# Layer 3's dense part: a chunk's attention values read from PSUM behind the last elementwise sum of the chunk ahead of it

## The chip, the cores and the metric

The kernel runs on one core of a Trainium2 chip. A core has engines that work side by side, each through its own queue of instructions: TensorE (PE in the profile; its weight loads are shown as PEld), VectorE (DVE), ScalarE (ACT), GpSimd (POOL), and SyncE (SP), which here only issues transfers. An engine starts its instructions in the order of its queue; one that waits for another engine holds back everything behind it. The metric is the device time of one execution in microseconds (us), lower is better. The number before is a median of 3 runs.

## The reference, cut to what matters

A graph of 2708 nodes with 512 features goes through four layers; each normalises the rows, clips them at zero, computes something over the graph and adds it to the rows. The change lies where layer 2 ends and layer 3 begins:

```python
    # --- layer 2 (adj_preln) ---
    h = jnp.maximum(_layernorm(x, axis=-1), 0.0)
    x = x + _L2_gnn_ref(h, adj, ...)       # attention with 8 heads of 64, softmax, then elu
    # --- layer 3 (adj_preln) ---
    h = jnp.maximum(_layernorm(x, axis=-1), 0.0)
    x = x + _L3_gnn_ref(h, adj, ...)
    # _L3: agg = mask @ x / max(deg, 1);  self_f = x @ W_self + b_self;  nb_f = agg @ W_nb + b_nb
    #      relu(concat([self_f, nb_f]) @ W_comb + b_comb)
```

The attention's weighted sums and the softmax's denominators are there at this point, transposed, in DRAM. What is left of layer 2 per node is the division, `elu`, and the addition to `x`; what begins of layer 3 is the normalisation and two products with 512x512 matrices (W_self and W_nb, each already multiplied by its half of W_comb).

## The kernel before, in words

The 2708 rows are cut into 22 chunks of 128 rows (the last has 20). The last part of layer 2 and the dense part of layer 3 are one software pipeline over these chunks, here called the dense loop. For a chunk c its steps are:

- `load3`: SyncE's queue loads the chunk's attention sums (aT), denominators (sT) and rows (x).
- `turn3`: TensorE multiplies sT into `sums_ps` (L1249) and transposes aT in four pieces into `av_ps` (L1253), both in PSUM. VectorE then makes the reciprocal denominators in four small instructions (`rs`, L1255 to L1258) and takes the attention values out of PSUM, multiplied by them, into `y` (L1260). These five are the instructions that the change touches.
- `elu3`: GpSimd makes z = min(y, 0) (L1267). VectorE adds max(y, 0) to the rows (L1268). ScalarE makes tanh(z/2) over y (L1270) and exp(z) over z (L1271); since exp(z) - 1 = (exp(z) + 1) tanh(z/2), VectorE multiplies these (L1272) and adds the product to the rows (L1273). L1273 is the last elementwise sum of a chunk: it completes layer 2.
- `save3`: ScalarE's queue stores the finished rows (L101).
- `normalize3`: VectorE takes mean and variance (L219, L221), ScalarE the square root (L223), VectorE its reciprocal (L225) and the normalised rows `hn` (L235).
- `transpose3`: TensorE transposes hn into PSUM (`hT_ps`, L246), ScalarE clips it at zero on the way out (L248).
- `nb3` and `self3`: TensorE multiplies hT with the two matrices (L187, eight matmuls of 512 columns each). Of nb3's result ScalarE takes the upper half of the bits (`halves`, L299), VectorE the rest (L300). To self3's result VectorE adds the bias (L1291), and ScalarE's queue stores it.

The first chunks run through these steps already between the last steps of the attention, by a plan that is written out by hand. The rest runs in this loop:

```python
        for c in range(1, NC):
            nb3(c)
            do(transpose3, c + 1)
            do(turn3, c + 3)
            do(normalize3, c + 2)
            do(save3, c + 2)
            do(elu3, c + 3)
            do(load3, c + 5)
            final = self3(c)
```

So at one time three chunks are in work on VectorE: c+3 comes out of the attention, c+2 gets its elu and its normalisation, c its product's halves. Square root on one side and tanh and exponential on the other need different tables on ScalarE, so each chunk has two loads of a table (shown as ACT_TABLE_LOAD); tanh is tied behind the newest square root by `issue_after(roots[-1])`.

The order in which one engine's instructions stand in its queue is not that of the source. The framework plays the program through before it runs, and gives an engine that becomes free the earliest traced instruction whose inputs are there by its own estimate of times. `tc.issue_after(ins)` is the means to correct this: what is traced within the block stands behind `ins` in the queue of `ins`'s engine. It adds an order, not a signal between engines. In the dense loop SBUF tiles of the pool `e3` (aT, sT, rs, y3, z3) have two buffers each, and PSUM eight banks.

Behind the dense loop comes the sum over the graph (`aggregate`, matmuls of L425), which runs to the end.

Of the kernel before, what the change touches and what calls it, by code (L numbers as in the profile page):

```python
# [15 lines left out]
ALU = mybir.AluOpType  # L16
# [6 lines left out]
R = 128  # L23
# [17 lines left out]
TINY = 1.0e-30  # L41
# [3 lines left out]
def fast_layers(  # L45
# [36 lines left out]
    nc = tc.nc  # L82
    N, D = x_in.shape
    H, _, O = w2.shape
# [876 lines left out]
    er = late.tile([R, NC, H], F32, name="er")  # L961
# [262 lines left out]
    tails_w = tails.tile([P, len(middle), O + S], F32, name="tails_w")  # L1224
    nc.gpsimd.memset(tails_w, 0.0)
    tails_f = tails.tile([P, 3], F32, name="tails_f")
    kept3, h3, l3_weights = {}, {}, []


    def load3(c):  # L1230
# [15 lines left out]
    def turn3(c):  # L1246
        xc, aT, sT = kept3[c]
        pr = ps.tile([P, 2, H], F32, name="sums_ps", tag="ps")
        nc.tensor.matmul(pr[:R], sT, mix[:NS], start=True, stop=True)  # L1249
        pt = ps.tile([P, H, O], F32, name="av_ps", tag="ps")  # L1250
        flat = pt.rearrange("p h o -> p (h o)")
        for k in range(NF):
            nc.tensor.transpose(flat[:R, k * P : (k + 1) * P], aT[:, k, :], ident)  # L1253
        rs = e3.tile([R, H, 1], F32, name="rs")
        nc.vector.tensor_tensor(rs[:, :, 0], er[:, c], pr[:R, 0], ALU.mult)  # L1255
        nc.vector.tensor_tensor(rs[:, :, 0], rs[:, :, 0], pr[:R, 1], ALU.add)
        nc.vector.tensor_scalar(rs[:, :, 0], rs[:, :, 0], TINY, None, op0=ALU.max)
        nc.vector.reciprocal(rs[:, :, 0], rs[:, :, 0])  # L1258
        y = e3.tile([R, H, O], F32, name="y3")
        nc.vector.tensor_tensor(y, pt[:R], rs.to_broadcast([R, H, O]), ALU.mult)  # L1260
        kept3[c] = xc, y.rearrange("p h o -> p (h o)")

    def elu3(c):

        xc, y = kept3[c]
        z = e3.tile([R, D], F32, name="z3")
        nc.gpsimd.tensor_scalar(z, y, 0.0, None, op0=ALU.min)  # L1267
        nc.vector.scalar_tensor_tensor(xc[:R], y, 0.0, xc[:R], op0=ALU.max, op1=ALU.add)  # L1268
        with tc.issue_after(roots[-1]):
            nc.scalar.activation(y, z, AF.Tanh, scale=0.5)  # L1270
            nc.scalar.activation(z, z, AF.Exp)  # L1271
        nc.vector.scalar_tensor_tensor(z, z, 1.0, y, op0=ALU.add, op1=ALU.mult)  # L1272
        nc.vector.tensor_tensor(xc[:R], xc[:R], z, ALU.add)  # L1273
        kept3[c] = xc

    def save3(c):
# [169 lines left out]
    for at_step, fn, c in (  # L1446
        (20, load3, 0),
        (19, load3, 1),
        (16, turn3, 0),
        (16, elu3, 0),  # L1450
        (15, load3, 2),
        (12, normalize3, 0),
        (12, save3, 0),
        (11, turn3, 1),
        (10, load3, 3),
        (10, elu3, 1),
        (7, normalize3, 1),
        (7, save3, 1),
        (6, transpose3, 0),
        (4, nb3, 0),  # L1460
        (4, turn3, 2),
        (3, self3, 0),
        (3, load3, 4),
        (3, elu3, 2),
        (2, transpose3, 1),
        (1, turn3, 3),
        (1, normalize3, 2),
        (1, save3, 2),
        (1, elu3, 3),
        (1, load3, 5),  # L1470
    ):
        behind(len(steps) - at_step, fn, c)
# [708 lines left out]
def kernel(tc: tile.TileContext, *args: bass.AP):  # L2181

    nc = tc.nc
    with tc.tile_pool(name="verdict", bufs=1) as pool:
        verdict = pool.tile([1, 1], I32, name="verdict")
        fast_layers(tc, *args, verdict)
        odd = nc.values_load(verdict[0:1, 0:1], min_val=0, max_val=P + 1)
        with tc.If(odd > 0):
            general_layers(tc, *args)
# [32 lines left out]
```

## Time and profile before

| | us |
|---|---|
| median of 3 runs | 1746.12 (1745.71 to 1747.05) |
| the profiled execution's own time | 1746.28 |
| its span, from the first to the last instruction | 1744.5 |
| TensorE busy in the span | 1721.5 |
| VectorE busy | 1317.9 |
| ScalarE busy | 845.4 |
| GpSimd busy | 248.3 |
| the dense loop, from its first product (nb3 of chunk 1) to the first matmul of the sum behind it | 1357.20 to 1522.14 |
| mean granted TensorE clock | 0.998 |

The busy shares are means over the whole kernel. The timeline gives an instruction's start, its duration, engine, line and names; in brackets the time that its engine stood idle before it, and what ended this. The chain of waits goes back from the last instruction through what released each step; it shows which engine's work followed on which, and where two engines take turns.

### The profile page before, as it was taken

The page shows a single profiled execution, that of the slowest core. Times are in us where ns is not written, and L with a number is a line of the kernel's source. Part 1 is how long each engine was busy: PE and PEld are TensorE (multiplying, and loading weights), DVE is VectorE, ACT ScalarE, POOL GpSimd, SP SyncE. Part 2 cuts the span into 40 slices and gives each one's busy share as a digit, 9 for nine tenths or more (in the row PEclk, how much of TensorE's full clock was granted, in tenths as well). Part 3 has the DMA queues.
Part 4 walks back from the last instruction along what each step waited for, and adds up shares of the span by engine and source line. Part 5 has one row for each costly group of instructions (what it writes and reads, how often), then busy time and mean ns, then how long its engine had stood idle before and what let it go on. Part 6 is the DMA issues. An engine that isn't in the chain of part 4 may idle for free.

```text
span 1744.5 us, 29430 instructions
## 1 busy us (share of the span) xinstructions
PE 1721.5 (99%) x11280; PEld 1074.9 (62%) x11280; DVE 1317.9 (76%) x1902; ACT 845.4 (48%) x1556; POOL 248.3 (14%) x252
## 2 busy tenths in 40 slices
PE   8999999999999999999999999999999999999998
PEld 5567777744458888644675665433434544588886
DVE  7759889865555556888899999999999787633334
ACT  5446767622210000266878888888794656400000
POOL 1003323311111111365000000000001222100000
PEclk9999999999999999999999999999999999999999
DMA  8446666444551111342420221022022444313221
GB/s 292 136 122 198 205 204 188 139 115 124 121 142 49 49 49 53 118 129 94 131 64 15 61 64 47 26 65 66 16 68 77 135 132 128 113 36 109 74 73 41
DMA packets 167227, 177.37 MB, mean 102 GB/s; under 512 B 84127, under 2 KB 106591, under 8 KB 166060
## 3 DMA queue, kind: packets, MB, share of 16 engines
q1 hardware_dynamic: 144428, 131.99, 27.4%
q10 hardware_dynamic: 18808, 33.37, 5.0%
q0 software_dynamic: 3840, 10.03, 1.5%
q8 instruction: 90, 1.47, 0.4%
q14 instruction: 61, 0.50, 0.1%
HBM read 111.64 MB, written 55.36 MB: 96 GB/s over the span
## 4 chain that ended last, share of the span: by engine, by line
PE 42%; DVE 9%; issue 3%; ACT 2%; DMA 2%; SPq 1%; POOL 0%; ACTq 0%; DVEq 0%; POOLq 0%
PE av L1315 15%; PE acc L425 12%; DVE t L1070 7%; PE self_ps L187 4%; PE nb_ps L187 4%; PE sums L1315 3%; DMA x<-x 1%; PE hT_ps L246 1%; PE wh_ps L187 1%; DVE wh_a L1117 1%; ACT b L1088 1%; PE av_ps L1253 1%; DVE f L1134 1%; DVE ln_st L219 0%; DMA rb<-rT 0%
## 5 line engine op out<-in xcount | busy, mean ns | idle before, releaser
L1070 DVE SCALAR_TENSOR_TENSOR t<-rb,ec,vT 128x2708 f32<-128x2708 f32 (+2 forms) x214 | 510.8, 2456 | 8.3 <-PE sums L1315 6.4
L1315 PE MATMUL av<-t,whs 128*32 128x451 f32 (+5 forms) x4432 | 444.6, 514 | 6.0 <-DVE t L1070 4.7
L425 PE MATMUL acc<-halves,kt 128*128 128x512 f32 x1848 | 423.6, 390 | 1.0 <-DVE kt L873 1.0
L425 PEld LDWEIGHTS acc<-halves,kt 128*128 128x128 f32 x1848 | 346.1, 188 | 75.3 <-DVE kt L873 2.6
L1088 ACT ACTIVATE b<-t,eb 128x2708 bf16<-128x2708 f32 (+1 forms) x119 | 285.1, 2396 | 33.2 <-DVE t L1070 33.1
L1315 PEld LDWEIGHTS av<-t,whs 128*32 128x32 f32 (+1 forms) x4432 | 192.4, 110 | 169.6 <-issue 119.4
L425 PE MATMUL acc<-halves,ar 128*128 128x512 f32 x924 | 243.8, 414 | 0.0
L425 PEld LDWEIGHTS acc<-halves,ar 128*128 128x128 f32 x924 | 172.5, 188 | 58.3 <-issue 20.8
L223 ACT ACTIVATE ln_rs<-ln_mv,eps 128x1 f32<-128x1 f32 x88 | 25.7, 295 | 305.9 <-DMA x<-x 199.0
L873 DVE SCALAR_TENSOR_TENSOR kt<-lastr,index,vT 128x512 fp32r<-128x512 int16 (+3 forms) x154 | 112.8, 747 | 72.4 <-PE acc L425 72.2
L1539 DVE CAST kt<-vT 128x512 fp32r<-128x512 uint8 (+3 forms) x154 | 56.4, 368 | 130.6 <-PE acc L425 130.6
L1267 POOL TENSOR_SCALAR z<-y 128x512 f32<-128x512 f32 x22 | 43.7, 1987 | 628.7 <-DVE y L1260 623.1
L558 DVE TENSOR_TENSOR_SCAN cum<-ai,deg 128x512 int16<-128x512 int32 (+2 forms) x110 | 128.3, 1170 | 0.0
L601 ACT ACTIVATE cum<-cum,limit 128x512 int16<-128x512 int16 (+3 forms) x132 | 88.0, 667 | 51.5 <-DVE deg L566 49.4
L1315 PE MATMUL sums<-t,whs 128*32 128x325 f32 (+4 forms) x952 | 103.9, 449 | 0.0
L1054 ACT ACTIVATE whs<-wh,ef 128x64 f32<-128x64 f32 x214 | 72.5, 341 | 53.0 <-PE sums L1315 18.9
L219 DVE BATCH_NORM_STATS2 ln_st<-x 128x6 f32<-128x512 f32 x88 | 60.5, 689 | 49.7 <-DMA x<-x 35.1
L187 PE MATMUL wh_ps<-w2s,hT 128*128 128x512 f32 x168 | 76.0, 595 | 0.9 <-ACT hT L248 0.9
L187 PE MATMUL h_ps<-w0s,hT 128*128 128x512 f32 x168 | 76.5, 598 | 0.0
L1315 PE MATMUL sums<-b,parts 128*32 128x338 bf16 (+2 forms) x884 | 76.2, 308 | 0.0
L552 ACT ACTIVATE ar<-ai 128x512 fp32r<-128x512 int32 (+2 forms) x132 | 75.0, 568 | 1.8 <-DMA ai<-in_adj 1.3
L187 PE MATMUL self_ps<-wfs,hT 128*128 128x512 f32 x168 | 75.7, 593 | 0.0
(211 smaller groups left out, 1956.2 us busy)
## 6 DMA issues: line engine op xcount, KB each, us to landing
x<-x SPq DMA_DIRECT2D x105, 256.0 KB
ai<-in_adj SPq DMA_DIRECT2D x84, 256.0 KB
x<-x ACTq DMA_DIRECT2D x84, 256.0 KB
x<-in_x SPq DMA_DIRECT2D x42, 256.0 KB
rb<-rT SPq DMA_DIRECT2D x7, 1354.0 KB
wh<-whd SPq DMA_DIRECT2D x63, 96.0 KB
packed<-two POOLq DMA_DIRECT2D x44, 128.0 KB, 3.0
whd<-wh SPq DMA_DIRECT2D x21, 256.0 KB
```

The costliest lines, as they stand in the source:

```text
L187: nc.tensor.matmul(po[:n], lhsT[:, f, :n], w[:, f, :], start=(f == 0), stop=(f == NF - 1))
L219: nc.vector.bn_stats(st[:n], xc[:n])
L425: nc.tensor.matmul(acc[:R], weight[:, k * R : (k + 1) * R], parts[:, i, :], start=(m == 0 and i == 0), stop=(m == NC - 1),)
L552: nc.scalar.activation(ar[:, :gw], ai[:, :gw], AF.Square, accum_out=squares[:R, m, g : g + 1])
L558: nc.vector.tensor_tensor_scan(cum[:n, :gw], ai[:n, :gw], ai[:n, :gw], 0.0 if g == 0 else deg[:n, m : m + 1], op0=ALU.add, op1=ALU.max,)
L601: nc.scalar.activation(cum[:n, :gw], cum[:n, :gw], AF.Sign, bias=limit[:n], scale=-1.0, accum_out=signs[:n, m, g : g + 1],)
L873: nc.vector.scalar_tensor_tensor(by_chunk(kt, cs), lastr[:, cs[0] * R : (cs[-1] + 1) * R].rearrange("p (c r) -> p c r", r=R), index[:R, m ...
L1054: ins = nc.scalar.activation(t[:q, :O], wh.pop((u, m))[:q], AF.Copy, scale=by)
L1070: ins = nc.vector.scalar_tensor_tensor(t[:q, : hi - lo], row[h][:q, lo:hi], ec[:q, m, h : h + 1], vT[g][:q, k, lo:hi], op0=ALU.max, op1=AL ...
L1088: nc.scalar.activation(b[:q, : hi - lo], weight[s][:, : hi - lo], AF.Sigmoid, bias=eb[:q, m, h : h + 1], scale=STEEP,)
L1315: nc.tensor.matmul(p[j * S : (j + 1) * S, : b - a], lhsT, rhs[:, part * size + a : part * size + b], start=(s % NC == 0), stop=(s % NC == ...
L1539: nc.vector.tensor_copy(by_chunk(kt, cs), pattern(m, cs))
```

## The change

The five VectorE instructions of `turn3` are put into an `issue_after` block behind the L1273 of the chunk before, for chunks 4 and up, which are those whose `turn3` stands in the loop above (18 chunks). The instruction is kept in a dictionary for this. Nothing is computed differently, no instruction is added or taken away, and no buffer changes.

```diff
-    kept3, h3, l3_weights = {}, {}, []
+    kept3, added, h3, l3_weights = {}, {}, {}, []
...
         rs = e3.tile([R, H, 1], F32, name="rs")
-        nc.vector.tensor_tensor(rs[:, :, 0], er[:, c], pr[:R, 0], ALU.mult)
-        nc.vector.tensor_tensor(rs[:, :, 0], rs[:, :, 0], pr[:R, 1], ALU.add)
-        nc.vector.tensor_scalar(rs[:, :, 0], rs[:, :, 0], TINY, None, op0=ALU.max)
-        nc.vector.reciprocal(rs[:, :, 0], rs[:, :, 0])
         y = e3.tile([R, H, O], F32, name="y3")
-        nc.vector.tensor_tensor(y, pt[:R], rs.to_broadcast([R, H, O]), ALU.mult)
+        with ExitStack() as behind:
+            if c > 3:
+                behind.enter_context(tc.issue_after(added[c - 1]))
+            nc.vector.tensor_tensor(rs[:, :, 0], er[:, c], pr[:R, 0], ALU.mult)
+            nc.vector.tensor_tensor(rs[:, :, 0], rs[:, :, 0], pr[:R, 1], ALU.add)
+            nc.vector.tensor_scalar(rs[:, :, 0], rs[:, :, 0], TINY, None, op0=ALU.max)
+            nc.vector.reciprocal(rs[:, :, 0], rs[:, :, 0])
+            nc.vector.tensor_tensor(y, pt[:R], rs.to_broadcast([R, H, O]), ALU.mult)
         kept3[c] = xc, y.rearrange("p h o -> p (h o)")
...
-        nc.vector.tensor_tensor(xc[:R], xc[:R], z, ALU.add)
+        added[c] = nc.vector.tensor_tensor(xc[:R], xc[:R], z, ALU.add).ins
```

## The prediction

> **What bounds the kernel now.** I read the page first: TensorE is busy for 99% of the span, so only an interval in which it stands, or starts late, can be won. I then took the chain of waits for the dense loop, then the waits of that stretch, then the timeline of one round of the loop. In the chain (start, us, what; `hT_ps` opens a round):
>
> ```profile
> 1368.55 0.44 PE hT_ps L246 x4
> 1368.99 0.13 PE sums_ps L1249 x2
> 1369.12 0.48 PE av_ps L1253 x4
> 1369.60 3.44 PE self_ps L187 x8
> 1373.04 3.43 PE nb_ps L187 x8
> 1376.47 0.44 PE hT_ps L246 x4
> ...
> 1433.49 0.03 issue
> 1433.53 0.66 PE hT_ps L246 x4
> 1434.18 0.13 PE sums_ps L1249 x2
> ```
>
> TensorE's own work for a chunk is 0.44 + 0.13 + 0.48 + 3.44 + 3.43 = 7.92 us, and two early rounds take just that (1360.63, 1368.55, 1376.47). From 1384 on a round takes 8.17: TensorE runs dry before the transposes of hn, a gap of 0.04, and four transposes that begin on an empty pipe last 0.66 instead of 0.44. The waits name the cause:
>
> ```profile
> PEld hT_ps L246 <- DVE hn L235: 12.1, 14, 0.9
> ```
>
> One round of VectorE up to hn (chunk 14 leaves the attention, 13 gets its elu and its normalisation; the brackets give idle time before):
>
> ```profile
> 1425.35 0.42 PEld L246 LDWEIGHTS hT_ps<-ident,hn 128*128 128x128 f32 x4 [0.86 <-DVE hn L235]
> ...
> 1426.18 0.16 DVE L1255 TENSOR_TENSOR rs<-er,sums_ps 128x8 f32<-128x8 f32 x1 [0.28 <-PE sums_ps L1249]
> ...
> 1427.08 0.69 DVE L1260 TENSOR_TENSOR y<-av_ps,rs 128x512 f32<-128x512 f32 x1
> ...
> 1427.81 0.69 DVE L1268 SCALAR_TENSOR_TENSOR x<-y,x 128x512 f32<-128x512 f32 x1
> ...
> 1428.42 1.10 DVE L1272 SCALAR_TENSOR_TENSOR z<-z,y 128x512 f32<-128x512 f32 x1
> ...
> 1430.04 0.67 DVE L1273 TENSOR_TENSOR x<-x,z 128x512 f32<-128x512 f32 x1
> ...
> 1432.92 0.55 DVE L235 TENSOR_SCALAR hn<-x,ln_mv,ln_rs 128x512 f32<-128x512 f32 x1
> ```
>
> The circle is closed: TensorE's hT of chunk 12 stands ahead of the sums of chunk 14; VectorE's rs of chunk 14 waits for those sums (0.28) and holds back L1272 of chunk 13, whose exponential (L1271, from 1426.50, 0.63) was ready at 1427.13 but which starts at 1428.42, behind y (L1260) and L1268; from L1273 on, the square root, its table and hn follow, and hn releases the next hT at 1433.53. That is 8.17 us, 0.25 more than TensorE needs.
>
> **What the Trainium skill says.** "TensorE: Matmul & The Clock Gate", section "Step-by-step: what each phase is for": matmuls stay in program order, only weight loads are pulled ahead. The trace agrees: the hT weight load is held for 0.86 us beside running matmuls, and sums and av follow it. "ScalarE: Activation LUTs", "What ACT_TABLE_LOAD costs": 1283 ns a switch, plus a drain of about 1380 ns. The trace has 1283 ns, but the next load starts 0.02 us after the square root, without such a drain, so I use 1.28. "SBUF — State Buffer", "SBUF: two separate sides": GpSimd and a VectorE instruction with two SBUF inputs exclude each other. The trace agrees: L1272 takes 1.10 beside GpSimd's z and 0.68 without it. "VectorE: DVE Perf Modes", "The DRAIN you can't avoid": a VectorE instruction that reads the one before needs a signal; in the trace dependent 512-wide ones start 0.71 to 0.73 apart, independent ones 0.60.
>
> **The change part by part.** No instruction is added. The dictionary costs nothing at run time. The order itself is on one engine; if it cost a wait instruction, the 21 ns shown for those on L1260, times 18 is 0.4 us, on a VectorE that would have slack. I take 0. No transfer is issued by the five moved instructions; the x, aT and sT loads on SyncE's queue wait for hn, av_ps and sums_ps as before, and the store of x on ScalarE's queue comes with L1273, so not later.
>
> *Removed.* L1272 no longer stands behind rs (0.90 from first start to y's), y (0.73 to L1268) and L1268 (0.61 to L1272), nor behind TensorE's sums. In the round shown it could start at 1427.2 instead of 1428.42.
>
> *Moved in.* Behind L1273 now come rs and y of the next chunk, in front of or between the statistics L219 and L221, which wait for L1273 themselves. The round at 1363 to 1366 shows such interleaving (L1273, rs, L219, y, L221, L1268), with starts 0.6 and 0.12 apart. From the start of L1273 as zero: rs 0.6, L219 0.7, rs 1.3, L221 1.45, the other two rs to 1.95, y 2.05 to 2.74. The square root does not suffer: its table is loaded 1.06 after L1273 starts (1390.23 against 1389.17) and done at 2.34, while L221 ends at 1.65. So sqrt ends at 2.65, the reciprocal follows at 2.7, hn at 3.4 to 3.9 if L1268 goes first, ending by 4.45. If all of rs and y stood ahead of L219 instead, L221 would end at about 3.0 and the root 0.7 later; below nothing this term cannot go, since the table sets the floor.
>
> *Late next: the elu of the chunk that was held back.* tanh writes over y, so it needs L1268 as well as z, and its table load waited for L1268 in front:
>
> ```profile
> 1359.67 1.28 ACT L1270 ACT_TABLE_LOAD   x1 [0.71 <-DVE x L1268]
> ```
>
> After y at 2.74, z takes 1.99 (to 4.78). L1268 starts at 2.8 and ends at 3.5, or 3.95 if GpSimd holds it (1.15 in one round). Then table 1.28, tanh 0.65, exp 0.65: done at 6.15 to 6.6, behind z in any case. L1272 then, L300 possibly between (0.60), and the next L1273 starts at 6.9 to 7.85. This new circle (L1273, y, L1268, table, exp, L1272, L1273) is my term for the round; I take 7.4 to 7.85, with L300 in between. It contains no TensorE result that is late: sums and av of a chunk are there 0.7 to 1.4 us after the nb product ends, and from that product's end to hn I count cast 0.6, L300 0.65, hn's end 4.45, some 5.7 of 7.92.
>
> *PSUM.* sums_ps and av_ps are held some 4 us longer each: about one bank more on average on top of 2.6 (21.6 us of bank time over 8.17, from the same round), of eight. I take 0; a wait would show at the nb or self product.
>
> *Sum.* Round = max(7.92, 7.4 to 7.85) = 7.92. The hT of chunk 4 starts at 1376.47 and that of chunk 20 ends at 1507.83, that is 131.36 us. Sixteen rounds of 7.92 and 0.44 are 127.16. The gain is 4.2 us, and it goes through to the end because behind 1507.83 the chain is TensorE alone up to the last elementwise steps at 1737. The span becomes 1744.5 - 4.2 = 1740.3; the profiled execution lies 1.78 above its span, so 1742.1; against the median 1746.12 it is 1741.9. I say 1742.0.
>
> **The rivals.**
>
> *A, the round is TensorE's 7.92 (chance 0.62):* 1742.0, own range 1741.3 to 1742.8. For it speak the rounds at 1360 and 1368, where L1272 and L1273 did stand ahead of y and L1268 and TensorE did not wait.
>
> *B, a circle a little above 7.92 (0.20):* hn in front of L1268 adds 0.5, the cast L299 between tanh and exp 0.5 (at 1361.50 it stands there); with either one the circle is 7.9 to 8.35. hn of chunk 4 was ready 1.7 us before its transpose; I count 1.2 of this left as a cushion. At 8.2 the loss is 16 x 0.28 - 1.2 = 3.3, a gain of 0.9: 1745.2. From 8.04 on the gain is under 3.5 us.
>
> *C, slower (0.18): the elu's round trip becomes the bound.* Place: ScalarE's table load in front of tanh, waiting for L1268, which now starts behind L1273, rs, y and hn. With both halves of a microsecond the circle is 8.4 to 8.85; at 8.65 the loss is 16 x 0.73 - 1.2 = 10.5 against 4.2 now: +6.3, 1752.4. It decides from 8.26 (no gain), and is over 0.2% slower from 8.48. Against it: this needs both unfavourable orders in every round.
>
> *That the order does not come out as written* would need L1272 to stay behind y for chunks 4 and up; the tie excludes it. *That hn was late for another reason*, the table load (1.28) for example, is excluded by the two early rounds, which had both table loads and no wait.
>
> **How the numbers follow.** A change of 0.2% (3.5 us) is about what a measurement of this kernel can tell from none. A's 4.2 is barely above it, so I give 0.02 of A to "within". Faster 0.60, within 0.22, slower 0.18. The range takes in A and B: from 1741.0 (A with 1 us of scatter) to 1749.6 (where C begins to be over 0.2%), leaving out C.
>
> **What the profile would show.** Right: hT_ps at 0.44 in the chain in nearly all rounds, starts 7.92 apart, no hn wait on the hT weight load, VectorE idle ahead of L1272. The order: L1273 ahead of L1255, then L219. Wrong: hT still at 0.66 with rounds of over 7.92, ScalarE idle ahead of the table load of L1270 with L1268 as releaser, or TensorE waiting for a PSUM bank ahead of a product.

## The result, and the profile after

The changed kernel takes 1741.51 us (median of 8 runs, 1741.19 to 1741.92), the kernel before 1746.19 (8 runs, 1745.45 to 1747.86): a ratio of 0.9974, 95% interval 0.9964 to 0.9983. That is 4.7 us, or 0.27%.

The chain of waits of the changed kernel in the dense loop (start, us, what):

```profile
1415.62 0.44 PE hT_ps L246 x4
1416.06 0.13 PE sums_ps L1249 x2
1416.18 0.48 PE av_ps L1253 x4
1416.67 3.44 PE self_ps L187 x8
1420.10 3.43 PE nb_ps L187 x8
1423.54 0.44 PE hT_ps L246 x4
```

Every round is now 7.92 us with hT_ps at 0.44, from the hT of chunk 2 (1360.18) to that of chunk 19 (1494.82); TensorE never runs dry in the loop. From the first nb product of chunk 0 to the first matmul of the sum behind the loop the timeline has 1342.52 to 1522.07 before and 1342.07 to 1517.41 after, that is 179.55 and 175.34 us: 4.21 us less. Nearly all the rest of the two spans' difference (1744.5 and 1739.8) is 0.45 us ahead of the loop, in a part that the change does not touch. I take it for a difference between two executions: over the profiles of all the kernels below, the loop's start lies anywhere between 1340.72 and 1343.47.

One round of VectorE in the timeline after (L1263 is y, L1271 the first addition, L1275 the product of the elu, L1276 the last sum; they were L1260, L1268, L1272 and L1273):

```profile
1423.02 0.69 DVE L1275 SCALAR_TENSOR_TENSOR z<-z,y 128x512 f32<-128x512 f32 x1 [1.35 <-ACT z L1274]
...
1424.19 0.69 DVE L300 TENSOR_TENSOR halves<-nb_ps,halves 128x512 fp32r<-128x512 f32 x1 [0.48 <-ACT halves L299]
...
1424.80 0.68 DVE L1276 TENSOR_TENSOR x<-x,z 128x512 f32<-128x512 f32 x1
1425.40 0.15 DVE L1259 TENSOR_TENSOR rs<-er,sums_ps 128x8 f32<-128x8 f32 x1
...
1425.52 0.69 DVE L219 BATCH_NORM_STATS2 ln_st<-x 128x6 f32<-128x512 f32 x1
...
1426.82 0.69 DVE L1263 TENSOR_TENSOR y<-av_ps,rs 128x512 f32<-128x512 f32 x1
...
1427.55 0.69 DVE L1271 SCALAR_TENSOR_TENSOR x<-y,x 128x512 f32<-128x512 f32 x1
...
1428.32 1.28 ACT L1273 ACT_TABLE_LOAD   x1 [0.85 <-DVE ln_rs L225]
```

The product (L1275) is now the first of its round, and VectorE stands idle 1.35 us ahead of it, waiting for the exponential. Ahead of L300 it waits for the cast L299, which waits for TensorE's nb product: the loop is paced by TensorE. Two more things are to be seen. L1275 takes 0.69 us where its counterpart before took 1.10. And the table load of tanh and the exponential now follows the first addition. (The bracket names L225, which ends 0.01 us before the load. But all 21 such loads of this trace start 0.07 to 0.08 us after the addition's end, also the first three, ahead of which L225 had ended 0.83 to 3.76 us earlier.)

### The profile page after: what moved, and what is told of

Read it like the earlier page. It is cut to its first block, busy times and chain, and to the rows that moved or that the text cites. A ratio compares the mean times of both kernels' runs of the same rounds, so it can differ in the third digit from the quotient of the medians.

```text
span 1739.8 us, 29452 instructions
## 1 busy us (share of the span) xinstructions
PE 1716.4 (99%) x11280; PEld 1078.0 (62%) x11280; DVE 1309.3 (75%) x1902; ACT 846.7 (49%) x1556; POOL 248.5 (14%) x252
## 4 chain that ended last, share of the span: by engine, by line
PE 87%; DVE 7%; ACT 2%; DMA 1%; issue 1%; SPq 1%; POOL 0%; ACTq 0%; DVEq 0%; POOLq 0%
PE acc L425 37%; PE av L1318 19%; PE nb_ps L187 8%; PE sums L1318 5%; PE h_ps L187 4%; PE self_ps L187 4%; PE line_ps L187 4%; DVE t L1070 4%; PE hT_ps L246 2%; PE fused_ps L371 2%; PE wh_ps L187 1%; DVE wh_a L1117 1%; PE av_ps L1253 1%; ACT b L1088 1%; DVE f L1134 1%
## 5 line engine op out<-in xcount | busy, mean ns | idle before, releaser
L219 DVE BATCH_NORM_STATS2 ln_st<-x 128x6 f32<-128x512 f32 x88 | 60.4, 688 | 48.6 <-DMA x<-x 34.4
```

The lines of the kernel that those rows point to most:

```text
L219: nc.vector.bn_stats(st[:n], xc[:n])
```

## The experiments

The lengths in this table are from the first nb product of chunk 0 to the first matmul of the sum behind the loop, by the timeline of each profile. Each ratio is to runs of the kernel before that were made beside it; their medians lie between 1745.67 and 1746.19, of which the first row gives one.

| kernel | median, us | ratio to before (95%) | loop, us |
|---|---|---|---|
| before | 1746.19 | | 179.55 |
| the change | 1741.51 | 0.9974 (0.9964 to 0.9983) | 175.34 |
| e1: only y tied | 1741.84 | 0.9975 (0.9965 to 0.9986) | 175.34 |
| e2: only the first addition tied | 1741.59 | 0.9973 (0.9963 to 0.9983) | 175.34 |
| e3: before, tanh twice | 1742.65 | 0.9979 (0.9971 to 0.9987) | 176.28 |
| e4: after, tanh twice | 1742.20 | 0.9976 (0.9967 to 0.9985) | 176.14 |
| e5: after, tanh three times | 1761.5 | 1.0093 (1.0076 to 1.011) | 195.19 |
| e6: after, tanh four times | 1767.77 | 1.0129 (1.0112 to 1.0145) | 201.81 |
| e7: rs and y behind hn | 1790.3 | 1.0257 (1.024 to 1.0274) | 222.59 |
| e8: before, z on ScalarE | 1742.32 | 0.998 (0.9973 to 0.9987) | 175.67 |
| e9: before, L300 ahead of the product | 1743.49 | 0.9985 (0.9978 to 0.9991) | 176.27 |
| e10: before, one more VectorE instruction | 1756.58 | 1.0061 (1.0047 to 1.0074) | 189.38 |
| e11: after, one more VectorE instruction | 1742.79 | 0.9984 (0.9978 to 0.9991) | 176.50 |

### Which part of the move counts: e1 and e2

e1 leaves rs where it was and ties only y:

```diff
-        with ExitStack() as behind:
-            if c > 3:
-                behind.enter_context(tc.issue_after(added[c - 1]))
-            nc.vector.tensor_tensor(rs[:, :, 0], er[:, c], pr[:R, 0], ALU.mult)
...
+        nc.vector.tensor_tensor(rs[:, :, 0], er[:, c], pr[:R, 0], ALU.mult)
...
+        with ExitStack() as behind:
+            if c > 3:
+                behind.enter_context(tc.issue_after(added[c - 1]))
             nc.vector.tensor_tensor(y, pt[:R], rs.to_broadcast([R, H, O]), ALU.mult)
```

> Only y (L1260 of before) is tied behind the sum L1273 of the chunk ahead; the four small rs instructions are left free. My theory (the elu of the chunk ahead no longer queues behind y and L1268): rs stays ahead of L1272 and still waits for TensorE's sums, but the circle over hn is 8.17 - 0.73 - 0.61 = 6.8 us, under TensorE's 7.92; 1741.5 as with the whole change, hT_ps at 0.44 in the chain. Rival 1 (the gain is that rs no longer makes VectorE wait for the sums, 0.28 a round): that wait is still there, so no gain, 1746. Rival 2 (the gain goes with the VectorE time moved out from ahead of L1272, 1.34 of 2.24 us): 1743.4.

e2 leaves rs and y free and puts the same block around the first addition in `elu3`:

```diff
+        with ExitStack() as behind:
+            if c > 3:
+                behind.enter_context(tc.issue_after(added[c - 1]))
-        nc.vector.scalar_tensor_tensor(xc[:R], y, 0.0, xc[:R], op0=ALU.max, op1=ALU.add)
+            nc.vector.scalar_tensor_tensor(xc[:R], y, 0.0, xc[:R], op0=ALU.max, op1=ALU.add)
```

> The kernel before, with only the addition L1268 tied behind the L1273 of the chunk ahead; rs and y stay ahead of L1272. My theory: the circle is 8.17 - 0.61 = 7.56 us, 0.36 under TensorE's 7.92, and a smaller move is as good as the whole: 1741.5 to 1742. Rival 1 (rs and its wait for the sums): no gain, 1746. Rival 2 (in proportion, 0.61 of 2.24 us): 1745.

Both have the whole gain and the same loop to 0.01 us. In the waits of e1 and e2 (from 1370 to 1500) rs still waits for TensorE's sums, even longer than the 0.28 us a round of before:

```profile
DVE rs L1256 <- PE sums_ps L1249: 27.6, 16, 1.7
```
```profile
DVE rs L1255 <- PE sums_ps L1249: 19.2, 16, 1.7
```

(e1 first, then e2: total us, times, longest.) So the wait for the sums is not what cost the time, and the gain does not go with the amount of work that is moved: 0.61 us out of the way is as good as 2.24. What I had not set apart from this is seen in the timeline of e2:

```profile
1424.82 0.69 DVE L1260 TENSOR_TENSOR y<-av_ps,rs 128x512 f32<-128x512 f32 x1
1425.43 0.68 DVE L1275 SCALAR_TENSOR_TENSOR z<-z,y 128x512 f32<-128x512 f32 x1
1425.60 1.86 POOL L1267 TENSOR_SCALAR z<-y 128x512 f32<-128x512 f32 x1 [6.06 <-DVE y L1260]
```

The product stands right behind y, starts 0.17 us ahead of GpSimd's z, and takes 0.68 us. The change, e1 and e2 all move something, but in all three the product also no longer takes the 1.10 us that it took before.

### Is ScalarE's elu the bound: e3 and e4

```diff
-            nc.scalar.activation(y, z, AF.Tanh, scale=0.5)
+            for _ in range(2 if c > 3 else 1):
+                nc.scalar.activation(y, z, AF.Tanh, scale=0.5)
```

> The kernel before, with tanh (L1270) issued twice for chunks 4 and up, 0.63 us more of ScalarE in each elu. My theory: before, the exponential was ready 1.3 us ahead of L1272, which queued behind y and L1268; the elu's round trip is not on the circle, so 1746 to 1747. Rival (ScalarE's two table loads a chunk are the bound of the loop): 18 x 0.63 = 11 us more, 1757.

> The changed kernel with the same 0.63 us more of ScalarE in each elu; the cast L299 comes to stand between tanh and exp, which adds 0.5. My theory: the elu's circle grows from some 6.9 to 7.9 us, just at TensorE's 7.92: 1741.5 to 1743. Rival (the change has made the elu's round trip the bound, or left no room): 18 x 0.63 = 11 us more, 1752.

e4 came as expected. e3 was a surprise: the kernel before became faster by 0.21% with 0.63 us more of work in each chunk. Both forecasts for e3, my theory's and the rival's, were wrong. The doubled tanh changed the planned order on VectorE: L300 came to stand between the first addition and the product. That pointed to the product's 1.10 us, and e8 and e9 were made to try it.

### The collision of the product with GpSimd: e8 and e9

Before, GpSimd's z starts 0.05 us after the first addition (1427.81), and the product stands right behind that addition (1428.42, 1.10 us):

```profile
1427.86 1.99 POOL L1267 TENSOR_SCALAR z<-y 128x512 f32<-128x512 f32 x1 [6.18 <-DVE y L1260]
```

e8 leaves VectorE's order as it was before and takes GpSimd out:

```diff
-        nc.gpsimd.tensor_scalar(z, y, 0.0, None, op0=ALU.min)
+        sign = -1.0 if c > 3 else 1.0
+        if c > 3:
+            nc.scalar.activation(z, y, AF.Relu, scale=-1.0)
+        else:
+            nc.gpsimd.tensor_scalar(z, y, 0.0, None, op0=ALU.min)
...
-            nc.scalar.activation(y, z, AF.Tanh, scale=0.5)
-            nc.scalar.activation(z, z, AF.Exp)
+            nc.scalar.activation(y, z, AF.Tanh, scale=0.5 * sign)
+            nc.scalar.activation(z, z, AF.Exp, scale=sign)
```

> The kernel before with GpSimd's min(y, 0) made on ScalarE for chunks 4 and up, as relu(-y), with the signs of tanh's and exp's scale turned; VectorE's order stays that of before, L1272 behind rs, y and L1268. New theory, from the runs so far: half a round's excess is a collision, L1272 held up 0.42 us by GpSimd's z (1.10 against 0.68); without it the circle is 8.17 - 0.42 = 7.75, under 7.92: 1741.5 to 1742.5, though no place in the queue has changed. First theory in its strict form (only L1272's place behind rs, y and L1268 costs): 1746.

The groups of the product between 1380 and 1495, the kernel before and then e8 (busy us, mean ns; then idle time before them):

```profile
L1272 DVE SCALAR_TENSOR_TENSOR z<-z,y 128x512 f32<-128x512 f32 x15 | 16.5, 1097 | 0.0
```
```profile
L1276 DVE SCALAR_TENSOR_TENSOR z<-z,y 128x512 f32<-128x512 f32 x14 | 9.6, 682 | 0.0
```

The product goes from 1.10 to 0.68 us in the same place of the queue, behind rs, y and the first addition, and 3.88 of the 4.21 us are won. The strict form of my theory, by which only the place costs, falls: it gave 1746, and 1742.32 was measured.

e9 keeps GpSimd's z and only puts L300 ahead of the product, by tracing the product one step later:

```diff
+    def join3(c):
+        z, y, xc = parts3.pop(c)
+        with ExitStack() as behind:
+            if c > 3:
+                behind.enter_context(tc.issue_after(low_half[c - 2]))
+            nc.vector.scalar_tensor_tensor(z, z, 1.0, y, op0=ALU.add, op1=ALU.mult)
+        nc.vector.tensor_tensor(xc[:R], xc[:R], z, ALU.add)
...
             nb3(c)
+            if 3 < c + 2 < NC:
+                join3(c + 2)
```

> The kernel before with L1272 traced a step later and tied behind L300, so that VectorE runs rs, y, L1268, L300, L1272, L1273 and nothing else changes. It is the order of the doubled tanh in the kernel before, without the doubled tanh. Collision theory: L300, which reads PSUM, covers GpSimd's hold, L1272 takes 0.68, L1273 comes 0.12 later behind its input: 8.17 - 0.42 + 0.12 = 7.87: 1741.5 to 1743. First theory (place behind rs, y, L1268): L1272 stands even later, 1746 or more.

```profile
1435.29 0.69 DVE L1270 SCALAR_TENSOR_TENSOR x<-y,x 128x512 f32<-128x512 f32 x1
1435.34 1.99 POOL L1269 TENSOR_SCALAR z<-y 128x512 f32<-128x512 f32 x1 [5.93 <-DVE y L1262]
1435.90 0.68 DVE L302 TENSOR_TENSOR halves<-nb_ps,halves 128x512 fp32r<-128x512 f32 x1
1436.50 0.68 DVE L1286 SCALAR_TENSOR_TENSOR z<-z,y 128x512 f32<-128x512 f32 x1
1437.22 0.69 DVE L1287 TENSOR_TENSOR x<-x,z 128x512 f32<-128x512 f32 x1
```

(L302 is the former L300, L1286 the product, L1287 the last sum.) The half of nb's product, which reads PSUM, runs its 0.68 us beside GpSimd, and the product behind it takes 0.68 too. It starts later after the first addition than before (1.21 us against 0.61), yet the last sum starts sooner: 1.93 us after the first addition against 2.23. That is 0.30 us, enough for a round that was 0.25 too long; 3.28 us are won in the loop. The median, 1743.49, lies 0.5 us above the range that I gave.

### Room on VectorE: e10 and e11

One more product whose result nobody reads, between the product of the elu and the last sum:

```diff
         nc.vector.scalar_tensor_tensor(z, z, 1.0, y, op0=ALU.add, op1=ALU.mult)
+        if c > 3:
+            nc.vector.tensor_tensor(y, z, z, ALU.mult)
```

> The kernel before with one more VectorE instruction per chunk from 4 on, a product of 128x512 between L1272 and L1273 whose result nobody reads. VectorE's circle is the bound here: 0.60 us more in each of 16 rounds, 9.6 us, 1755 to 1756. Rival (VectorE has room, the bound is elsewhere): under 1748.

> The changed kernel with the same further instruction. In the trace after, hn is ready 2.3 us before its transpose, and the elu's circle is 7.4 us; with 0.6 more it is 8.0, at the bound: 1741.5 to 1743. It also bears on whether the change would do without the end of the collision, since 0.6 is more than the 0.42 that this is worth. Rival (VectorE's circle is still the bound): 9.6 us more, 1751.

The kernel before becomes 9.83 us longer in the loop; 16 rounds of 0.60 are 9.6. (Its median is 0.6 us above the range that I gave.) Its transposes, in the timeline of e10, start 8.77 apart, behind hn:

```profile
1438.38 0.65 PE L246 MATMUL hT_ps<-ident,hn 128*128 128x128 f32 x4 [0.64 <-DVE hn L235]
...
1447.15 0.66 PE L246 MATMUL hT_ps<-ident,hn 128*128 128x128 f32 x4 [0.63 <-DVE hn L235]
```

The changed kernel takes the same instruction for 1.16 us in all. Its first rounds stay at 7.92, the later ones at 7.96 (hT at 1472.52 and 1480.47). So VectorE's circle was the bound before and is not after: 7.96 with the added 0.60 puts it at 7.36, under TensorE's 7.92. Two conclusions follow, of unequal strength. The end of the collision is enough without the move: e8 shows it. The move would be enough without the end of the collision: that is an estimate, 7.36 + 0.42 = 7.78, and no run moves the values and keeps the product at 1.10.

### How far the values may be taken back: e5, e6 and e7

e5 and e6 repeat tanh three and four times in the changed kernel.

> The changed kernel with tanh issued three times for chunks 4 and up. My theory: the circle L1273, y, L1268, table, three tanh with the clipping L248 between them, exp, L1272, L1273 is some 8.5 us, over TensorE's 7.92: 16 x 0.58 less a cushion of 1.2 is 8 us more, 1747 to 1752, hT_ps at 0.66 again and TensorE waiting for hn. Rival (the loop has more room than I count): still 1741.5 to 1743.

> The changed kernel with tanh issued four times. My theory: each further tanh adds 0.63 us a round once the circle is over 7.92, so about 10 us more than with three: 1757 to 1762. Rival (still room): under 1750.

The turn from room to none came between two and three, as expected, but both times are outside the ranges that I gave: e5 lost 20 us where I gave 8, and the fourth tanh cost 6.3 where I gave 10. In the timeline of e5:

```profile
1438.06 0.69 DVE L1271 SCALAR_TENSOR_TENSOR x<-y,x 128x512 f32<-128x512 f32 x1
...
1438.89 0.59 ACT L299 CAST halves<-nb_ps 128x512 fp32r<-128x512 f32 x1 [0.92 <-PE nb_ps L187]
...
1439.49 1.28 ACT L1274 ACT_TABLE_LOAD   x1
...
1439.64 0.63 PE L246 MATMUL hT_ps<-ident,hn 128*128 128x128 f32 x4 [0.79 <-DVE hn L235]
```

The cast L299 now stands ahead of the table load and waits for TensorE's nb product. Without it the load could start at 1438.83, behind the first addition; it starts at 1439.49. That adds 0.66 us to my circle of 8.5 in this round and 0.36 in the next (1448.39 against 1448.03), and closes it over TensorE, which waits for hn in turn: two rounds take 18.1 us, 9.05 each. With a fourth tanh (9.38 a round) half of the 0.63 is spent where the cast had been waiting: ScalarE stands idle 0.28 and 0.60 us ahead of the cast in two rounds of e6, 0.62 and 0.92 in two of e5.

e7 traces `turn3` behind `normalize3` and ties rs and y behind hn:

```diff
-                behind.enter_context(tc.issue_after(added[c - 1]))
+                behind.enter_context(tc.issue_after(normed[-1]))
...
-            do(turn3, c + 3)
             do(normalize3, c + 2)
+            do(turn3, c + 3)
```

> The changed kernel with rs and y tied not behind L1273 but further back, behind the hn (L235) of the chunk ahead; turn3 is traced after normalize3 for this. My theory: L1273 to hn is 3.45 us, then rs, y, L1268, table, tanh, exp, L1272, L1273 one after the other, with y_self and L300 in between: a circle of some 10 us, so 16 x 2.1 - 1 = 33 us more than the change, 1766 to 1780. Rival (only the order of L1273 against y and L1268 counts, anything behind it is as good): 1741.5.

Slower by 2.57%, 49 us above the change, more than the 33 I gave. The chain of e7 shows the circle that I had named, and TensorE's products in it as well:

```profile
1427.13 0.55 DVE hn L235
...
1427.82 1.09 PE hT_ps L246 x4
...
1430.08 4.05 PE self_ps L187 x8
1434.13 3.45 PE nb_ps L187 x8
...
1437.60 0.59 ACT halves L299
...
1438.22 0.69 DVE halves L300
...
1439.26 0.70 DVE y L1263
1439.98 0.70 DVE x L1271
...
1440.75 1.28 ACT L1273
```

L300 stands ahead of y in VectorE's queue and waits, over the cast, for the product that hn released; two rounds take 20.85 us (hT at 1406.97 and 1427.82). My 33 us also left out TensorE itself: hT takes 1.09 us in this chain and the self product 4.05, where the changed kernel has 0.44 and 3.44. TensorE has stood for 3.15 us ahead of this hT; from 1427.80 to 1430.10 its granted clock is 0.50, and over the whole loop 0.92, against 1.00 in the loops of the kernels before and after, e5, e6 and e10. In e6, where TensorE waits 1.54 us at most and the clock stays at 1.00, it is busy for 178.76 us of the loop; in e7 for 193.55. These 15 us are about what my 33 were short by. That the long wait brings the lower clock down on it is likely from this order of events, but no run sets it apart. So the place behind the last sum is one of a few good ones, and a place further back costs ten times what the change wins.

## Why the prediction was right, point by point

The time, 1742.0, was 0.5 us off, with the case I held for likeliest.

- **TensorE's 7.92 as the floor, and 16 rounds to win: right.** The loop became 4.21 us shorter; I gave 4.2. The other 0.5 us of the difference of medians is not explained by the loop.
- **No transfer, no bank, no wait added: right.** Nothing of the kind stands in the chain or in the waits of TensorE after.
- **"Moved in", counted from the start of the last sum: right but for one instruction.** rs at 0.60, L219 at 0.72, y at 2.02, the first addition at 2.75, the square root done at 2.66, the table load at 3.52, hn at 3.55. The reciprocal of the root came at 3.36 and not at 2.7, since the first addition stood ahead of it; the room of 2.3 us ahead of the transpose hid this.
- **"Late next", the elu's circle of 7.4 to 7.85: right, at its lower end.** The exponential was done 6.16 us after the last sum's start. With the product's 0.6 and L300's 0.6 the circle is 7.4. VectorE waits for the cast there, so the round is TensorE's. e11 confirms the size: with 0.6 us more the rounds took 7.96. One detail is closer than foreseen: tanh waits for its table and for GpSimd's z, and these end together, at 1429.60 and 1429.59, so a faster table load alone would win nothing there.
- **"Removed" was half of the cause.** I read the product's delay as queueing behind rs, y and the first addition, and took its 1.10 us as given, although the prediction itself set it beside 0.68. The excess of a round was 0.25 us. The end of the collision takes 0.42 us out of the circle, the place behind the first addition 0.61 by the distance of the two starts: either one covers the excess. e8 and e9 show this for the collision without the move; for the move without the end of the collision it is the estimate from e11. The change does both, and so the time came out right although I had named only one.
- **Rival C, the elu's round trip as the bound: did not come in the change, but e5 and e6 show that it is real.** It begins between one and two further tanh, as the expectation of e5 has it. The price in that expectation was too small, since it left out the cast ahead of the table load. Of the two orders that rival B feared, hn ahead of the first addition and the cast between tanh and exp, neither came in the changed kernel; the second came in e4, whose rounds stayed at 7.92 up to the last two.
- **The chance of "within 0.2%"** was put at 0.22, because 4.2 us was barely above 3.5. The measured interval, 0.17% to 0.36%, includes 0.2%.
- **What neither the prediction nor a run tried.** The circle before has one more term that could go. Between the end of the last sum (1430.71) and the table load for the square root (1431.10) ScalarE's queue issues the store of the rows (1430.74, 0.33 us), and the root, at 1432.39, waits for that load and not for its variance, which was done at 1431.65. With the store on another queue up to 0.36 us might be saved, more than the excess; this is an estimate from these times, and not shown.

## What to carry to other kernels

In a loop over several engines, write down the period of each closed circle, not the load of each engine: here VectorE was idle for over a microsecond in every round (1.07 and 0.28 us in the one shown) and still set the pace, and each run that took more than 0.25 us out of its circle won, whether by a move or by the end of the collision. When an instruction is longer in one place than in another, count the difference as a part of the excess before looking at the queue. And an order that is fixed by a tie has a best place: behind the last sum nothing was lost, behind the normalisation 49 us were, some 15 of them in a slower TensorE.

## What the runs showed of the hardware and the planner that was not expected

- A GpSimd instruction that starts beside VectorE's first addition holds up the VectorE instruction with two SBUF inputs that stands right behind it, by 0.42 us (1.10 against 0.68 in e8, which has no such GpSimd instruction), although its own record is 1.99 us long. Put 0.6 us later, the same instruction is not held at all while GpSimd's record still runs (e9: 1436.50 to 1437.18, with GpSimd's from 1435.34 to 1437.33). An instruction with one input in PSUM in between is not held either. VectorE's hn, which reads one large tensor from SBUF, took 0.64 us beside GpSimd's z after the change, and 0.55 before, where z was not running.
- TensorE's granted clock can fall within a loop: 0.50 from 1427.80 to 1430.10 of e7, behind a wait of 3.15 us. No such fall came in e5 and e6, with waits of at most 1.54 us.
- Work that is added can make a kernel faster: two tanh instead of one in the kernel before gave 0.9979 (0.9971 to 0.9987), because the planner, by its own times, then ordered VectorE's queue another way. e9 has that order with a single tanh, and its loop is as long: 176.27 against 176.28 us.
